# End of cross attention in a decoder: the first local row prepared in single pieces, and the last projections in the scores' PSUM

## The chip, the cores and the metric

The kernel runs on one core of one Trainium2 chip. The metric is device time in microseconds. The kernel before took a median of 3036.18 us over three runs (3035.45 to 3040.28).

## The reference, cut to what matters

Two decoder layers work on x with 8 batch rows of 512 tokens and 256 channels. The change lies between the second and the third block of the first layer:

```python
x = x + _L0_attn_ref(_layernorm(x), ...)            # self attention
x = x + _L0_xattn_ref(_layernorm(x), ctx_1024, ...) # cross attention, 16 heads of 16
x = x + _L0_ffn_ref(_layernorm(x), ...)             # local transformer: 2 x (local attention, FFN)
```

Cross attention: queries from x and keys and values from the context; a masked softmax with a factor exp(adj); an output projection; and the sum with x. The local transformer that follows takes a fresh layer norm of that sum. Each of its layers shifts half of the channels by one token and projects to q, k, v (8 heads of 64). It divides each head of q and k by its own length, turns them by rotary angles with scales, attends in windows of 128 keys, and projects back. A gated FFN follows. All arithmetic is in float32.

## The kernel before, in words

`FastDecoder` (from L1278) writes the whole program out, one stage after another, and each stage is a generator. A stage runs its first pieces while the stage ahead of it is still at work: `Ahead.step(k)` advances it by k `yield`s, until it yields `MAIN`. Then its main part begins, with PSUM pools of its own. `Background` (L3366) is a heap of small thunks with due times; `later.tick(2)` runs up to two that are due.

The program is written in this order, but a scheduler decides in which order the instructions stand on each engine. It goes by readiness and by the program's order as priority, and by when tile slots come free. `tc.issue_after(ins)` puts what a block writes behind `ins`, for the instructions of the same engine as `ins` only. `paced(thunk)` (L1707) does so with `marks[-2]`, the last multiplication on VectorE (DVE) of two steps ago. Once it is laid out, each engine works strictly in order, and so does the DMA queue of SyncE (SP). A DMA that waits holds up those behind it.

**Cross attention** (`stage_cross_attention`, L1528) runs 128 steps, 16 for each batch row: step i is four heads against 128 keys. `scores(i)` (L1724) makes four matmuls on TensorE (PE) into two tiles of two PSUM banks each (tag "sc", three such tiles). `soften(i)` takes the exponential of both tiles on ScalarE (ACT, L1735) and multiplies them by mask and adj on DVE (L1736). `weigh(i - 2)` (L1752) makes eight matmuls against the values into the bank "po". After every fourth step `po` is copied out as `x_o` (L1758, ACT). Four DMAs bring it to `x_oT` (L1766). Its sums go through DRAM to `x_sums` (L3302, L3303); `x_inv` is their reciprocal (L3306, DVE); this goes through `invs` (L3307) to `x_wide` (L1776, four DMAs). GpSimd (POOL) multiplies `x_oT` by `x_wide` (L1769). When the second group of a row is there, `project_out(b, i)` follows for four token tiles: two matmuls (L1785) into the bank "pj", an addition to x (L1790, DVE), and its statistics (L1495, L1496). After the fourth, x is written to DRAM (`away`, L1797). Newton steps for the reciprocal root (L1506 to L1508) and the normalization in place (L157) come then. The last waits for the write to `away`, since it overwrites x.

The PSUM of this stage is full: one bank "pj", one "po", six for "sc".

**Local attention's first row** is prepared during the last steps of cross attention (`prepare(0)` in `local_attention`, L1836): rotary tables, then

- `turn` (L1873): transpose x, copies on ACT into `la_hT`;
- `project(i, j)` (L1889): two matmuls for token tile i and part j (0 q, 1 k, 2 v); for q and k two reads by ACT (L1896 square, L1897 copy), for v one copy (L1894);
- `square` (L1905, DVE): sums of squares; `root` (L1913 and L1477 to L1481, DVE): 11 small instructions for two tiles;
- `rotate` (DVE): normalization (L1920), two halves with sine (L1928, L1929), cosine (L1930), sum (L1931);
- `turn_heads` (L1939, PE; L1942, ACT): transposes into `la_qkT`, in two halves of four.

All these write PSUM through `self.pj()`, which is the one bank "pj" until local attention's own pools exist. These pools lie on the same eight banks: "sum" and "po" first, then four banks of scores where the first two "sc" tiles were, then two "pj" where the third was.

The main part of local attention then begins with `scores` (L2007), whose results DVE adds a mask to (L2016), and with `prepare(1)`.

In the kernel before, the list of pieces has 18 thunks, of up to three calls each; from step 116 on, `ahead.step(3)` writes three of them per step, with no `paced` around it.

Of the kernel before, what the change touches and what calls it, by code (L numbers as in the profile page):

```python
# [27 lines left out]
F32 = mybir.dt.float32  # L28
# [6 lines left out]
ALU = mybir.AluOpType  # L35
# [4 lines left out]
P = 128  # L40
B, S, C = 8, 512, 256
# [1236 lines left out]
class FastDecoder(Decoder):  # L1278
# [249 lines left out]
    def stage_cross_attention(self, ahead):  # L1528
# [6 lines left out]
        nc, t = self.nc, self.t  # L1535
# [6 lines left out]
        first = early.enter_context(self.tc.tile_pool(reuse_waits="tile", name="xa0", bufs=2, side="right"))  # L1542
# [154 lines left out]
        with self.tc.tile_pool(reuse_waits="tile", name="xa", bufs=2) as pool, self.tc.tile_pool(  # L1697
# [9 lines left out]
            def paced(thunk):  # L1707

                with self.tc.issue_after(marks[-2]):
                    thunk()  # L1710

            def scores(n):
                b, rest = divmod(n, 16)
                G, kt = divmod(rest, 4)
                g, e = divmod(G, 2)
                d = held[b]
                d.setdefault("e", {})[rest] = pair = []
                for p in range(2):
                    pair.append(self.alloc(psum, [P, 2, 512], F32, "sc", bufs=3))

                for m in self.together(4):
                    r = (m + 2) % 4
                    rows = slice(32 * r, 32 * r + 32)
                    nc.tensor.matmul(  # L1724
                        pair[r // 2][:, r % 2, :], d["k"][rows, g, kt * P : (kt + 1) * P], d["q"][rows, e, g, :],
                        start=True, stop=True,
                    )

            def soften(n):
                b, rest = divmod(n, 16)  # L1730
                kt = rest % 4
                d = held[b]
                for p in range(2):
                    ex = self.alloc(pool, [P, 2, 512], F32, "x_e", bufs=6)
                    nc.scalar.activation(ex, d["e"][rest][p], AF.Exp)  # L1735
                    nc.vector.tensor_tensor(  # L1736
                        ex, ex, d["share"][:, kt, :].unsqueeze(1).broadcast_to([P, 2, 512]), ALU.mult
                    )
                    d["e"][rest][p] = ex
                marks.append(self.newest(mybir.EngineType.DVE))  # L1740
# [41 lines left out]
            def project_out(b, i):  # L1782
# [13 lines left out]
                if i == NST - 1:  # L1796
# [3 lines left out]
                    for k, normal in enumerate(normals):  # L1800
                        later.add(5 + k // 2, lambda normal=normal: paced(normal))

            n = 16 * B
            ready = None
            for i in range(n + 2):
                if i < n:
                    if i % 16 == 0:
                        ready = prepare(i // 16 + 1) if i // 16 + 1 < B else iter(())
                    scores(i)
                    soften(i)  # L1810
                if i >= 2:
                    weigh(i - 2)

                for thunk in next(ready, ()):
                    if len(marks) > 1:
                        paced(thunk)
                    else:
                        thunk()
                later.tick(2)
                if i == 1:  # L1820
                    ahead.step()
                if i == n - 14:
                    early.close()
                if i >= n - 12:
                    ahead.step(3)
            ahead.step(100)
            later.drain()

    def residual(self, pool, b):
        x = self.alloc(pool, [P, NST, C], F32, "lf_x")
# [3 lines left out]
    def local_attention(self, l, y, ahead):  # L1836
# [3 lines left out]
        nc, t = self.nc, self.t  # L1840
# [6 lines left out]
        first = early.enter_context(self.tc.tile_pool(reuse_waits="tile", name="la0", bufs=2, side=sides[0]))  # L1847
# [8 lines left out]
        for i in range(NST):  # L1856
            c, s = tab["cos"][:, i], tab["sin"][:, i]
# [55 lines left out]
            nc.vector.tensor_scalar(ss, ss, 1e-24, None, ALU.max)  # L1913
            self.rsqrt(first, rn, ss, "la_rt")

        def rotate(b, i):
            d = held[b]
            qk, rn = d["rows", i], d["rn"][:, i % 2, :]
            q3 = qk.rearrange("p (h d) -> p h d", d=64)
            nc.vector.tensor_tensor(  # L1920
                q3, q3, rn.unsqueeze(2).broadcast_to([P, 16, 64]), ALU.mult
            )
            q4 = qk.rearrange("p (j h d) -> p j h d", j=2, d=64)
            r = self.alloc(first, [P, 2 * S], F32, "la_r", bufs=1)
            r4 = r.rearrange("p (j h d) -> p j h d", j=2, d=64)
            cos = tab["cos"][:, i].unsqueeze(2).broadcast_to([P, 2, 8, 64])
            sin = tab["sin"][:, i].unsqueeze(2).broadcast_to([P, 2, 8, 64])
            nc.vector.tensor_tensor(r4[..., :32], q4[..., 32:], sin[..., :32], ALU.mult)  # L1928
            nc.vector.tensor_tensor(r4[..., 32:], q4[..., :32], sin[..., 32:], ALU.mult)  # L1929
            nc.vector.tensor_tensor(q4, q4, cos, ALU.mult)  # L1930
            nc.vector.tensor_tensor(qk, qk, r, ALU.add)  # L1931

        def turn_heads(b, i):
            d = held[b]
# [12 lines left out]
        def prepare(b):  # L1947

            def one(*calls):
                def thunk():  # L1950
                    for f, *args in calls:
                        f(b, *args)
                return thunk

            p, t, s, r = project, turn_heads, square, rotate
            return [
                [one((turn, 0)), one((turn, 1)), one((p, 0, 0)), one((p, 0, 1), (s, 0))],
                [one((p, 1, 0)), one((p, 1, 1), (s, 1), (root,))],
                [one((p, 2, 0), (r, 0)), one((p, 2, 1))],
                [one((p, 3, 0), (r, 1)), one((p, 3, 1))],  # L1960
                [one((p, 0, 2), (s, 2)), one((t, 0), (s, 3), (root,))],
                [one((p, 1, 2), (r, 2)), one((t, 1))],
                [one((p, 2, 2), (r, 3)), one((t, 2))],
                [one((p, 3, 2)), one((t, 3))],
            ]
# [3 lines left out]
        for thunks in prepare(0):  # L1969
            for thunk in thunks:  # L1970
                thunk()
                yield
        yield Ahead.MAIN

        with self.tc.tile_pool(
# [4 lines left out]
            one, two = [P, 512], [P, 2, 512]  # L1980
# [97 lines left out]
            n = 8 * B  # L2078
            ahead.step()
            for pair in range(0, n + 2, 2):  # L2080
                if pair < n:
                    if pair % 8 == 0:
                        ready = prepare(pair // 8 + 1) if pair // 8 + 1 < B else [()] * 8
                    scores(pair // 2)
                if pair >= 2:
                    weigh(pair // 2 - 1)
                for i in (pair, pair + 1):
                    with self.in_turn():
                        later.tick(1)
                    if i < n:  # L2090
                        for thunk in ready[i % 8]:
                            with self.in_turn():
                                thunk()
                                later.tick(1)
                    if i == n - 6:
                        early.close()
                    if i > n - 6:
                        with self.in_turn():
                            ahead.step()
# [1477 lines left out]
```

## Time and profile before

| What | Value |
|---|---|
| median of three runs | 3036.18 us |
| profiled execution, its own time | 3039.56 us |
| span of that execution | 3037.8 us |
| PE busy | 2832.6 us (93%) |
| DVE busy | 2039.3 us (67%) |
| ACT busy | 1191.5 us (39%) |
| PE busy from 600 to 700 us | 77.64 us, granted clock 0.82 |
| PE busy from 500 to 600 us | 94.48 us, granted clock 1.00 |
| PE busy from 700 to 800 us | 93.25 us, granted clock 0.97 |

In a row of the profile, a group has the engine, the line of the kernel, the operation, what is written and what is read, and the count. A bracket holds the idle time ahead of it on its engine and who ended that idle time. A granted clock of 1.00 means that TensorE had all its pulses; at 0.50 a matmul takes twice as long. In the table by stretches, the busy time of an engine can hold part of a wait, when the wait belongs to the instruction. "Row 6" and "row 7" below are the last two batch rows of cross attention; "row 0" and "row 1" are the first two of local attention.

### The profile page before, as it was taken

How to read it: one execution, taken by the hardware profiler on the slowest of the kernel's cores; microseconds unless marked ns; L12 is line 12 of the kernel's file. 1: busy time of each engine (PE TensorE's matmuls, PEld its weight loads, DVE VectorE, ACT ScalarE, POOL GpSimd, SP SyncE). 2: the span in 40 equal slices, each digit the busy share in tenths (PEclk: the TensorE clock that was granted, in tenths of full speed). 3: DMA queues.
4: the chain of work that ended last, by engine and by line, in shares of the span. 5: the costliest groups of instructions: out<-in, count | busy, mean ns of one | idle time of the engine just before them, and what ended most of it. 6: DMA issues, size and time to landing. Idle time of an engine off the chain costs nothing. (4 is left out here: it accounts for less than half of the span.)

```text
span 3037.8 us, 39774 instructions
## 1 busy us (share of the span) xinstructions
PE 2832.6 (93%) x14929; PEld 1511.4 (50%) x14944; DVE 2039.3 (67%) x4546; ACT 1191.5 (39%) x1687; POOL 388.1 (13%) x357
## 2 busy tenths in 40 slices
PE   8999999979999999999999989998796999997998
PEld 5653333225555556555555556564444344444665
DVE  7458998977776784356776788548797766664110
ACT  2237776744444431124444431113364444441111
POOL 1111111100011110000101111101211012121111
PEclk9999999988999999999999999999897999997999
DMA  7011212101000011001000011001332132313331
GB/s 246 1 35 50 72 51 62 42 18 57 15 23 23 15 32 36 0 1 37 22 22 17 21 46 63 21 7 63 106 132 91 43 105 78 112 58 97 102 140 61
DMA packets 130694, 168.71 MB, mean 56 GB/s; under 512 B 51761, under 2 KB 79666, under 8 KB 128443
## 3 DMA queue, kind: packets, MB, share of 16 engines
q1 hardware_dynamic: 126394, 154.48, 16.3%
q0 software_dynamic: 4096, 11.59, 1.0%
q8 instruction: 119, 1.95, 0.3%
q14 instruction: 85, 0.69, 0.1%
HBM read 113.12 MB, written 47.50 MB: 53 GB/s over the span
## 5 line engine op out<-in xcount | busy, mean ns | idle before, releaser
L1889 PE MATMUL pj<-w,la_hT 128*128 128x512 f32 x720 | 334.2, 605 | 5.2 <-ACT la_qkT L1942 4.5
L1736 DVE TENSOR_TENSOR x_e<-x_e,x_share 128x1024 f32<-128x1024 f32 x256 | 315.9, 1277 | 14.3 <-ACT x_e L1735 14.1
L1735 ACT ACTIVATE x_e<-sc 128x1024 f32<-128x1024 f32 x256 | 249.2, 1023 | 83.8 <-PE sc L1724 83.8
L1889 PEld LDWEIGHTS pj<-w,la_hT 128*128 128x128 f32 x720 | 132.6, 191 | 153.4 <-issue 115.6
L2016 DVE TENSOR_TENSOR la_e<-sc,la_mask 128x1024 f32<-128x1024 f32 (+1 forms) x128 | 135.3, 1084 | 103.6 <-PE sc L2007 103.6
L3320 POOL TENSOR_TENSOR la_oT<-la_o,x_wide 128x512 f32<-128x512 f32 x64 | 97.7, 1538 | 753.1 <-DMA x_wide<-invs 678.6
L2945 ACT ACTIVATE ma_e<-sc,ma_bias 128x1024 f32<-128x1024 f32 x128 | 135.6, 1110 | 145.9 <-PE sc L2939 131.4
L2233 ACT ACTIVATE lf_gate<-pj,lf_b 128x512 f32<-128x512 f32 (+1 forms) x82 | 56.3, 687 | 333.3 <-PE pj L2212 318.0
L2020 ACT ACTIVATE la_e<-la_e 128x1024 f32<-128x1024 f32 (+1 forms) x128 | 117.5, 946 | 152.6 <-DVE la_e L2016 151.6
L2212 PE MATMUL pj<-lf_hnT,w 128*128 128x512 f32 (+1 forms) x368 | 171.4, 593 | 2.0 <-DVE lf_hid L2238 2.0
L1752 PE MATMUL po<-x_e,x_v 128*32 128x512 f32 x1024 | 140.7, 622 | 33.7 <-DVE x_e L1736 29.7
L2212 PE MATMUL sc<-lf_hnT,w 128*128 128x512 f32 x336 | 157.7, 592 | 0.0
L1724 PE MATMUL sc<-x_q,x_k 32*128 32x512 f32 x1024 | 152.9, 647 | 1.7 <-DVE sa_ok L1448 1.4
L2284 PE MATMUL po<-w,lf_hid 128*128 128x256 f32 x640 | 149.0, 379 | 0.0
L2238 DVE SCALAR_TENSOR_TENSOR lf_hid<-sc,lf_b,lf_gate 128x512 f32<-128x512 f32 x70 | 52.4, 749 | 136.4 <-PE sc L2212 133.4
L2027 PE MATMUL po<-la_e,la_v 128*64 128x256 f32 (+1 forms) x1024 | 125.8, 370 | 7.0 <-ACT la_o L2044 6.3
L2007 PE MATMUL sc<-la_qkT 64*128 64x256 f32 (+1 forms) x1024 | 128.9, 375 | 1.2 <-DVE la_e L2016 0.6
L2284 PEld LDWEIGHTS po<-w,lf_hid 128*128 128x128 f32 x640 | 117.8, 190 | 21.2 <-issue 7.4
L2939 PE MATMUL sc<-ma_qT,ma_kT 64*128 64x512 f32 x512 | 127.3, 615 | 0.4 <-ACT ma_e L2945 0.4
L2962 PE MATMUL po<-ma_e,ma_v 128*64 128x512 f32 x512 | 125.7, 612 | 0.0
L2070 PE MATMUL pj<-w,la_oT 128*128 128x256 f32 x512 | 121.0, 383 | 2.0 <-DVE lf_t L1480 0.7
L1905 DVE TENSOR_REDUCE la_ss<-la_sq 128x16 f32<-128x1024 f32 x64 | 77.7, 1215 | 65.8 <-ACT la_sq L1896 65.8
(500 smaller groups left out, 5173.6 us busy)
## 6 DMA issues: line engine op xcount, KB each, us to landing
x_wide<-invs SPq DMA_DIRECT2D x184, 128.0 KB
w<-in_f_w_dram SPq DMA_DIRECT2D x16, 1024.0 KB
kv<-kv_o SPq DMA_DIRECT2D x56, 256.0 KB
slots<-x_empty SPq DMA_DIRECT2D x8, 1028.0 KB
x_mask<-in_x_maskT_dram SPq DMA_DIRECT2D x8, 1024.0 KB
ma_kT<-kv SPq DMA_DIRECT2D x8, 1024.0 KB
ma_v<-kv SPq DMA_DIRECT2D x8, 1024.0 KB
ex_rows<-slots SPq DMA_DIRECT2D x7, 1028.0 KB
```

Of the source, the lines that this page charges most:

```text
L1724: nc.tensor.matmul(pair[r // 2][:, r % 2, :], d["k"][rows, g, kt * P : (kt + 1) * P], d["q"][rows, e, g, :], start=True, stop=True,)
L1735: nc.scalar.activation(ex, d["e"][rest][p], AF.Exp)
L1736: nc.vector.tensor_tensor(ex, ex, d["share"][:, kt, :].unsqueeze(1).broadcast_to([P, 2, 512]), ALU.mult)
L1752: nc.tensor.matmul(d["po"][32 * r : 32 * r + 32, :], d["v"][:, kt, 8 * g + 2 * r + e, :], ex[r // 2][:, r % 2, :], start=(kt == 0), stop=( ...
L1889: nc.tensor.matmul(ps, d["hT"][:, k, i * P : (i + 1) * P], wqkv[:, k, j * S : (j + 1) * S], start=(k == 0), stop=(k == 1),)
L2007: nc.tensor.matmul(both[half][:, r, jj * 256 : jj * 256 + to - j * P], d["qkT"][rows, 4 + c, j * P : (j + 1) * P], d["qkT"][rows, c, j * P ...
L2016: nc.vector.tensor_tensor(ex[:, :, :n_cols], ps[:, :, :n_cols], mask[:, :n_cols].unsqueeze(1).broadcast_to([P, 2, n_cols]), ALU.add,)
L2027: nc.tensor.matmul(out[:, j * P : to], lhsT(j), ex[:, jj * 256 : jj * 256 + to - j * P], start=(j == 0), stop=(j == 3), skip_group_check=True,
L2212: nc.tensor.matmul(ps[:m, :], w1[:, k, at : at + m], held[b]["hnT"][:, k, :], start=(k == 0), stop=(k == 1))
L2284: nc.tensor.matmul(ps[:, :C], held[b]["hid"][:, f, i * P : (i + 1) * P], w2[:, f, :], start=(f == 0), stop=False,)
L2939: nc.tensor.matmul(both[m // 2][:, r, :], d["k"][rows, c, kt * P : (kt + 1) * P], d["q"][rows, c, :], start=True, stop=True,)
L2945: nc.scalar.activation(ex, ps, AF.Exp, bias=bias[:, b * NST + kt : b * NST + kt + 1], scale=0.125)
```

## The change

There are three parts, all in the last steps of cross attention.

1. `prepare(0)` of the first local attention gives 36 thunks of one call each in a new order. A rotation is cut in three calls: normalization, the two sine halves, and cosine with sum.
2. The pieces are written from step 115 on, not 116: two per step, not three. They stand inside `paced`, so that their DVE instructions stand behind the multiplication of two steps ago.
3. From step 127 on, `self.pj()` gives a slot of the tag "pj" once in four times, and a tile of the tag "sc" (its first half) the other three times.

```diff
+            turns = iter(range(10**6))
+            def at_end():
+                if next(turns) % 4 == 0:
+                    return self.alloc(psum, [P, 512], F32, "pj")
+                return self.alloc(psum, [P, 2, 512], F32, "sc", bufs=3)[:, 0, :]
...
-                if i >= n - 12:
-                    ahead.step(3)
+                if i >= n - 13:
+                    paced(lambda: ahead.step(2))
+                if i == n - 1:
+                    self.pj = at_end
...
-        def rotate(b, i):
+        def rotate(b, i, pieces=(0, 1, 2)):
...
+            if 0 in pieces:
+                nc.vector.tensor_tensor(
+                    q3, q3, rn.unsqueeze(2).broadcast_to([P, 16, 64]), ALU.mult
+                )
+            if 1 in pieces:
+                d["r"] = self.alloc(first, [P, 2 * S], F32, "la_r", bufs=1)
+                r4 = d["r"].rearrange("p (j h d) -> p j h d", j=2, d=64)
+                nc.vector.tensor_tensor(r4[..., :32], q4[..., 32:], sin[..., :32], ALU.mult)
+                nc.vector.tensor_tensor(r4[..., 32:], q4[..., :32], sin[..., 32:], ALU.mult)
+            if 2 in pieces:
+                nc.vector.tensor_tensor(q4, q4, cos, ALU.mult)
+                nc.vector.tensor_tensor(qk, qk, d["r"], ALU.add)
...
+            if b == 0 and l == 0:
+                calls = [
+                    (turn, 0), (turn, 1), (p, 0, 0), (p, 0, 1), (p, 1, 0), (s, 0), (p, 1, 1), (s, 1), (root,),
+                    (p, 2, 0), (r, 0, (0,)), (p, 2, 1), (r, 0, (1,)), (p, 3, 0), (r, 0, (2,)), (p, 3, 1),
+                    (r, 1, (0,)), (t, 0), (r, 1, (1,)), (s, 2), (p, 0, 2), (r, 1, (2,)), (s, 3), (root,),
+                    (t, 1), (r, 2, (0,)), (p, 1, 2), (r, 2, (1,)), (p, 2, 2), (r, 2, (2,)), (r, 3, (0,)),
+                    (p, 3, 2), (t, 2), (r, 3, (1,)), (r, 3, (2,)), (t, 3),
+                ]
+                return [[one(call)] for call in calls]
```

`p`, `t`, `s` and `r` are `project`, `turn_heads`, `square` and `rotate`; the first number is the token tile.

## The prediction

> **What bounds the kernel at this place.** I read the windows table first, by tens of microseconds over the hand-over from cross attention to the first local attention. Columns: stretch, length, then busy time of PE, PE weight loads, DVE, ACT, POOL, then the granted TensorE clock, DMA share and GB/s.
>
> ```profile
> 620.00:630.00 10.00, 10.00 (x57) 2.77 (x56) 9.59 (x19) 7.98 (x12) 0.00 (x0) 1.00 0.06 15
> 630.00:640.00 10.00, 6.36 (x28) 1.82 (x24) 10.00 (x11) 5.92 (x8) 0.00 (x0) 1.00 0.00 1
> 640.00:650.00 10.00, 9.32 (x40) 2.78 (x40) 9.62 (x19) 3.69 (x5) 0.00 (x0) 0.66 0.05 12
> 650.00:660.00 10.00, 3.87 (x25) 0.79 (x21) 9.97 (x9) 2.43 (x3) 1.67 (x1) 0.86 0.07 19
> ...
> 680.00:690.00 10.00, 7.90 (x17) 4.69 (x16) 4.98 (x18) 0.00 (x0) 0.76 (x4) 0.50 0.09 36
> 690.00:700.00 10.00, 8.46 (x23) 5.04 (x22) 6.39 (x27) 0.00 (x0) 0.00 (x0) 0.50 0.14 34
> ```
>
> Three regimes are visible. Up to 630 PE is full: one step of the loop (scores, one projection, weighting) every 3.98 us. From 630 to about 665 DVE is full and PE is not: DVE is the limit. From 665 to 700 neither is: that is a chain. The timeline of PE shows the second and third regime row by row (start, length, work; in brackets the idle time ahead of it and who ended it):
>
> ```profile
> 628.26 1.06 PE L1752 MATMUL po<-x_e,x_v 128*32 128x512 f32 x8
> ...
> 633.81 1.06 PE L1752 MATMUL po<-x_e,x_v 128*32 128x512 f32 x8 [1.50 <-DVE x_e L1736]
> ...
> 640.68 1.94 PE L1752 MATMUL po<-x_e,x_v 128*32 128x512 f32 x8 [2.82 <-DVE x_e L1736]
> ...
> 658.12 1.94 PE L1752 MATMUL po<-x_e,x_v 128*32 128x512 f32 x8 [6.13 <-DVE x_e L1736]
> ...
> 665.03 1.07 PE L1752 MATMUL po<-x_e,x_v 128*32 128x512 f32 x8
> ...
> 678.00 2.07 PE L1785 MATMUL pj<-w,x_oT 128*128 128x256 f32 x4 [0.68 <-ACT la_qkT L1942]
> 680.59 2.07 PE L1785 MATMUL pj<-w,x_oT 128*128 128x256 f32 x4 [0.51 <-DVE x L1790]
> ...
> 696.13 2.07 PE L1785 MATMUL pj<-w,x_oT 128*128 128x256 f32 x4 [0.52 <-DVE x L1790]
> 698.13 3.36 PE L2007 MATMUL sc<-la_qkT 64*128 64x256 f32 x16
> ```
>
> The weighting waits for the x_e multiplication, which stands on DVE behind whole rotations. After the last weighting (665.03), the eight output projections of rows 6 and 7 go one by one through the single pj bank, 2.59 us each at half clock: 8 x 2.59 = 20.1 us, from 678.00 to 698.13. And local attention starts still later, as the timeline of DVE shows:
>
> ```profile
> 706.35 1.39 DVE L157 TENSOR_SCALAR x<-x,lt_ln_mean,lt_ln_rstd 128x256 f32<-128x256 f32 x4 [4.77 <-DMA away<-x]
> 707.65 1.22 DVE L1905 TENSOR_REDUCE la_ss<-la_sq 128x16 f32<-128x1024 f32 x1
> 708.78 2.08 DVE L2016 TENSOR_TENSOR la_e<-sc,la_mask 128x1024 f32<-128x1024 f32 x2
> ```
>
> So the end of this stage is 708.78, the first mask addition L2016. It stands on DVE behind row 7's normalization, which waits for the write to `away`, issued when the last projection has been added.
>
> **The change, part by part.** I take the order in which the changed kernel's instructions stand on each engine and fill it with the durations above. The instructions are the same ones; behind the start of local attention the order is the same on all engines; on POOL it is the same throughout. So only this window counts. Start is common: DVE reaches the x_e pair at 605.92 in both, behind the rotary tables, whose wait for la_scale (2.22 us) stays, because the DMAs stand alike on SP up to there.
>
> Step lengths used, each from back-to-back starts: x_e pair 2.28 (1.14 each), square sum 1.13, root 11 x 0.225 = 2.47, rotation 1.14 + 2 x 0.60 + 2 x 1.14 = 4.6, projection of the local row 1.92, weighting or scores 1.0 to 1.07, row projection L1785 1.06 at full clock and 2.07 at half.
>
> *1. Up to 628.* The local row's first transposition moves one step earlier. It fills PE's idle 2.60 us at 601 to 604, but the weightings still run at 3.98 us a step, so 628.26 stays: worth 0. If PE were not the limit there it would be worth up to 1.9.
>
> *2. The last six weightings.* Before: 628.26 to 665.03, 36.8 us. In the new order DVE gives, from the pair at 617.5 (the reciprocal ahead waits until 615.0 for its sums, as now): pair 619.8, square 620.9, root 623.4, normalization 624.5, pair 626.8, rotation 630.3, pair 632.6, normalization and reciprocal 633.9, pair 636.2, two sines 637.4, and only then L1790 of row 6's first projection, 637.8. That last one is the new wait. Row 6's four projections now stand inside the loop, in the single pj bank, and the bank is emptied by DVE, in order. Behind it on PE stand the local projection, the next scores, and all after them: PE idles 633.7 to 637.9, 4.2 us. It comes back with the third such projection, behind a rotation, a square and a root: 650.2 to 655.1, 4.9 us. The other two wait under 1 us. At full clock the last weighting then starts at 659.1, six us earlier than now.
>
> Here the clock decides. The Trainium skill (TensorE: Matmul & The Clock Gate, Part 1: The HAM clock gate) says that one idle window of about 3.4 us puts the array at half clock, until about 3.4 us of work release it. This speaks against the change: both new gaps are longer. The trace goes further: the gap of 2.82 us already gave a weighting of 1.94 in place of 1.06, and half clock to 647; the one of 6.13 gave 5.7 us of it. So by the rows both gaps cost: local projection +1.9, scores +1.0 behind the first; projection +1.9, weighting +0.9, L1785 +1.0 behind the second. Sum +6, last weighting at about 665.5. With gaps under the rule it would be 659.1. I take 665.5 because 4.2 and 4.9 lie between two gaps that both halved it; so this part is worth 0 (6 at most, -4 if half clock lasts to the end).
>
> *3. Behind the last weighting.* Now: x_o ends 666.74; reciprocal 673.06 (it waits for DMA); POOL multiplies at 677.93, 4.87 later; then the 20.1 us. In the new order, from x_o at 666.8: row 7's four projections use separate banks, and their first halves are done ahead. On SP `away` of row 6 stands behind the first of four x_oT copies, but its addition is done (665.7), so nothing waits. The reciprocal, though, now stands on DVE behind the last two rotations without normalization, row 6's statistics and its normalization: 665.7 + 9.6 = 675.3; `away` is issued at 667.3 and lands 5.5 later (688.32 to 693.87 now), 672.8, so it is hidden, by 2.5 us; four L157 at 0.34, then the reciprocal at 676.8, 3.7 later than now. Multiplication 676.8 + 4.87 = 681.7, end 682.9. Four closing matmuls at half clock, 2.07/4 each: 685.0; last addition 686.0 (now 698.66). Row 7's DMA to `away` as now, behind w1's load, 698.72 to 706.35 = 7.6, and 0.3 to issue: 693.9. L157 1.3 and square 1.13 as now: L2016 at 696.4 against 708.78, **12.4 us less**. The square's own input, two projections of the next row, is ready 4.6 us after their start at about 688, so it is covered by 1 us.
>
> Row 6's four additions, statistics and Newton steps (about 8.5 us on DVE) move from a time when DVE had nothing to do (6.80 and 1.49 us waits) to one when it is the limit; steps 2 and 3 contain that.
>
> *4. Afterwards.* PE is 92 to 96% busy in each 100 us from 700 to 1100, in the same order; loads are issued by the work, so the shift carries on. Unknown: 2 us either way, from where a clock window falls.
>
> Sum against its own execution: 3039.56 us, span 3037.8, gives 3027.1 and 3025.4. That execution is 3.4 above the median of the three runs, 3036.18; the saving is applied to the median: 3036.18 - 12.4 = 3023.8, with half a microsecond for a clock that recovers between the gaps: **3023.3**.
>
> **The rivals.** *A, clock stays up* (0.12): the gaps come out shorter, since a DVE row may overlap more. Last weighting 659.1, x_o 660.8, last rotation 670.3, reciprocal 671.7, L2016 691.5: 17.3 us less, 3019. For it: PE is full between the gaps. Against: the two rows of 1.94.
>
> *B, half the gain* (0.17): the pj bank costs more. Each of four hand-overs that slips by one x_e pair and a root piece, about 1.5 us, takes 6 us: 3030. For it: two of four already wait over 4 us. Against: later ones have DVE work that was due anyway.
>
> *C, no change* (0.07): the end is given by something not in this count, for instance DVE catching up with row 1's rotations (DVE is full at 720 to 730), so that an early start is waited away: 3034 to 3038. Against: that work is the same and starts with the same event.
>
> *D, slower* (0.06): the same hand-over, one mechanism. From 628 on PE runs through six weightings with four projections whose bank DVE must empty. If each costs more than 3.1 us beyond the count (4 x 3.1 = 12.4), the gain is gone; at 5 us, as when each addition stands behind a full rotation or root and the array stays at half clock, it is 20 us, 3044. For it: the order does put additions behind such pieces twice. Against: the DVE work up to the last x_e multiplication is about 4 us less than now (one and a half rotations moved behind it, additions added), so PE cannot be held longer than DVE is full.
>
> **How the numbers follow.** My case has 0.58, 3018 to 3027. Three runs lie within 4.8 us, so about 0.2% (6 us) can be told from no change. Faster: 0.58 + 0.12 + nearly all of B = 0.86; same: C and the edge of B, 0.08; slower 0.06. Range 3015 to 3031: A's 3019 less 2 and a bit, B's end; C and D stay out.
>
> **What would show it.** L1785 of row 6 between the last weightings; two PE gaps of 4 to 5 us ahead of local projections, ended by DVE L1790, half clock behind both; last weighting at 665; eight serial projections gone; reciprocal of row 7 near 677, L2016 near 696. Wrong if the last weighting is past 675, or if the reciprocal waits for `away`, or if local attention's next row is not ready.

## The result and the profile after

The changed kernel takes 3024.47 us (median of 9 runs, 3020.36 to 3029.2) against 3036.18 us beside it (9 runs, 3030.28 to 3041.62): ratio 0.996, 95% interval 0.995 to 0.9971, that is 11.7 us less by the medians. Forecast were 3023.3 us: 12.4 us less by the sum, and half a microsecond more as an allowance for the clock. The profiled execution takes 3023.1 us, span 3021.3, which is 16.5 us below the profiled execution of before. So the size is right, but the profiled pair differs by 4 us more than the sum had it, and that has to be explained too.

The windows table of the changed kernel comes first (columns as in the table of before: stretch, length, busy time of PE, weight loads, DVE, ACT, POOL, granted clock, DMA share, GB/s):

```profile
630.00:640.00 10.00, 4.31 (x12) 1.33 (x12) 10.00 (x14) 0.63 (x1) 1.72 (x1) 0.67 0.06 14
640.00:650.00 10.00, 9.91 (x65) 3.61 (x64) 7.66 (x10) 8.42 (x11) 0.42 (x1) 0.98 0.07 17
650.00:660.00 10.00, 6.08 (x24) 2.16 (x24) 9.09 (x22) 0.69 (x2) 0.00 (x0) 0.83 0.07 14
660.00:670.00 10.00, 9.17 (x45) 4.88 (x38) 9.79 (x26) 4.45 (x9) 0.10 (x1) 1.00 0.20 67
670.00:680.00 10.00, 4.92 (x17) 3.50 (x15) 2.67 (x10) 1.02 (x2) 2.75 (x6) 0.72 0.08 16
680.00:690.00 10.00, 9.71 (x40) 5.32 (x39) 4.85 (x23) 3.71 (x7) 0.00 (x0) 0.94 0.78 264
690.00:700.00 10.00, 8.69 (x45) 4.63 (x44) 9.25 (x19) 7.11 (x12) 0.00 (x0) 1.00 0.00 0
```

The three regimes are there again. DVE is full to nearly full from 630 to 670, with one slack stretch (7.66 from 640). What is gone is the long time at clock 0.50: before had it from 680 to 700, and behind 660 there is now only the stretch from 670 that is low (0.72). The two low stretches ahead (0.67 and 0.83) hold the gaps of the next table. The burst of loads for the next stage (264 GB/s) stands at 680; before it came at 700.

The timeline of PE in the changed kernel (start, length, work; the bracket holds the idle time ahead and who ended it):

```profile
626.49 1.07 PE L1752 MATMUL po<-x_e,x_v 128*32 128x512 f32 x8
...
631.72 1.06 PE L1752 MATMUL po<-x_e,x_v 128*32 128x512 f32 x8 [2.03 <-DVE x_e L1736]
636.75 3.74 PE L1897 MATMUL pj<-w,la_hT 128*128 128x512 f32 x4 [3.97 <-DVE x L1790]
640.42 1.14 PE L1724 MATMUL sc<-x_q,x_k 32*128 32x512 f32 x8
...
654.07 3.61 PE L1897 MATMUL pj<-w,la_hT 128*128 128x512 f32 x4 [3.92 <-DVE x L1790]
657.62 1.06 PE L1752 MATMUL po<-x_e,x_v 128*32 128x512 f32 x8
...
659.67 1.07 PE L1752 MATMUL po<-x_e,x_v 128*32 128x512 f32 x8
...
676.86 1.22 PE L1785 MATMUL sc<-w,x_oT 128*128 128x256 f32 x2 [5.08 <-POOL x_oT L1769]
...
678.72 1.91 PE L1785 MATMUL sc<-w,x_oT 128*128 128x256 f32 x4
680.57 2.12 PE L2027 MATMUL sc<-la_qkT 64*128 64x256 f32 x16
```

The two hand-overs of the pj bank show as gaps of 3.97 and 3.92 us, both ended by the addition L1790. Half clock covers just the one projection behind each (3.74 and 3.61 in place of 1.98). The next scores (1.14) and the next weighting (1.06) are at full clock again; in the two later profiles of this kernel these rows take up to 0.23 us longer. Between the end of GpSimd's multiplication (676.80) and the first scores of local attention there are now 3.7 us of closing projections (676.86 to 680.57); eight serial projections, one every 2.59 us, stood there before. The timeline of DVE shows the chain around it:

```profile
669.28 1.38 DVE L157 TENSOR_SCALAR x<-x,lt_ln_mean,lt_ln_rstd 128x256 f32<-128x256 f32 x4
670.57 0.25 DVE L3326 RECIPROCAL x_inv<-x_sums 128x16 f32<-128x16 f32 x1
...
680.68 0.42 DVE L1790 TENSOR_TENSOR x<-x,sc 128x256 f32<-128x256 f32 x1
688.76 1.38 DVE L157 TENSOR_SCALAR x<-x,lt_ln_mean,lt_ln_rstd 128x256 f32<-128x256 f32 x4 [4.73 <-DMA away<-x]
690.05 1.21 DVE L1913 TENSOR_REDUCE la_ss<-la_sq 128x16 f32<-128x1024 f32 x1
691.18 2.08 DVE L2036 TENSOR_TENSOR la_e<-sc,la_mask 128x1024 f32<-128x1024 f32 x2
```

Row 6's normalization (669.28) has no wait in brackets: its write to `away` has landed. The reciprocal of row 7 stands right behind it. The end of the stage, the first mask addition, is at 691.18 in place of 708.78.

Whole executions start this window up to 4 us apart, so the runs below are compared from a common mark: the seventh weighting from the end (626.49 here, 628.26 in before), the last row up to which PE is full in every kernel. Times from that mark, each from the kernel's timelines, "third scores" being the third group of L2027 (L2007 in before):

| Kernel | last weighting | reciprocal of row 7 | first mask addition | third scores | whole profiled execution |
|---|---|---|---|---|---|
| before | 36.77 | 44.80 | 80.52 | 92.24 | 3039.56 |
| before, second profile | 35.69 | 43.70 | 80.99 | 92.71 | 3042.36 |
| changed | 33.18 | 44.08 | 64.69 | 76.41 | 3023.10 |
| changed, second profile | 33.84 | 44.75 | 65.28 | 76.99 | 3024.27 |
| changed, third profile | 33.52 | 44.43 | 65.20 | 76.92 | 3025.91 |
| PSUM alone | 35.48 | 43.49 | 74.88 | 86.60 | 3032.04 |
| pieces alone | 33.53 | 44.43 | 71.26 | 82.98 | 3027.04 |
| unpaced | 36.28 | 46.41 | 65.73 | 77.45 | 3028.43 |
| additions first | 34.52 | 44.75 | 63.86 | 75.57 | 3021.39 |
| `away` first | 33.61 | 44.52 | 59.65 | 75.80 | 3022.54 |
| reciprocal first | 33.65 | 41.99 | 61.77 | 73.49 | 3016.64 |
| reciprocal first, second profile | 33.88 | 42.22 | 61.63 | 73.34 | 3023.55 |
| reciprocal and `away` first | 33.60 | 41.94 | 56.82 | 72.58 | 3017.98 |
| all three | 34.45 | 43.74 | 58.20 | 73.70 | 3022.65 |

Profiles of the same kernel lie up to 1.1 us apart in the first two columns and up to 0.6 in the next two, so smaller differences between two rows say nothing.

The reciprocal of row 7 comes at the same time in before and after, for different reasons. In before, DVE stood idle until its sums had come; in the changed kernel it stands right behind other work of DVE (669.28 above). The row of before:

```profile
673.06 0.25 DVE L3306 RECIPROCAL x_inv<-x_sums 128x16 f32<-128x16 f32 x1 [7.99 <-DMA x_sums<-sums]
```

All the gain, 80.76 - 65.06 = 15.7 us on the means, comes behind this reciprocal.

### The profile page after: what moved, and what is told of

The parts are those of the page before. It is cut to its first block, busy times and chain, and to the rows that moved or that the text cites. A ratio compares the mean times of both kernels' runs of the same rounds, so it can differ in the third digit from the quotient of the medians.

```text
span 3021.3 us, 39786 instructions
## 1 busy us (share of the span) xinstructions
PE 2819.4 (93%) x14944; PEld 1507.2 (50%) x14944; DVE 2034.0 (67%) x4546; ACT 1192.4 (39%) x1687; POOL 386.9 (13%) x357
## 5 line engine op out<-in xcount | busy, mean ns | idle before, releaser
L2027 PE MATMUL sc<-la_qkT 64*128 64x256 f32 (+1 forms) x1024 | 128.0, 373 | 2.5 <-DVE la_e L2036 1.9
```

The lines of the kernel that those rows point to most:

```text
L2027: nc.tensor.matmul(both[half][:, r, jj * 256 : jj * 256 + to - j * P], d["qkT"][rows, 4 + c, j * P : (j + 1) * P], d["qkT"][rows, c, j * P ...
```

## The experiments

My theory: PSUM banks for row 7 and pieces behind the multiplications each carry part of the gain. The rivals: one of the two parts does all, the clock decides, or DVE's work alone sets the end whatever the order.

### The PSUM part alone

The kernel before with only the third part of the change:

```diff
+            turns = iter(range(10**7))
+            def at_end():
+                if next(turns) % 4 == 0:
+                    return self.alloc(psum, [P, 512], F32, "pj")
+                return self.alloc(psum, [P, 2, 512], F32, "sc", bufs=3)[:, 0, :]
...
                 if i >= n - 12:
                     ahead.step(3)
+                if i == n - 1:
+                    self.pj = at_end
```

> The kernel before, and only the last part of the change: from step 127 on, pieces that ask for a bank get the scores' PSUM three times in four. Theory (the gain comes from taking the eight output projections out of one bank behind the last weighting): row 6 still goes one by one through pj, 4 x 2.59 us, row 7 no longer: the first local scores start near 690.5 in place of 698.1, the time is 7 to 8 us under the kernel before. Rival (the gain comes from the single pieces, which free DVE for the x_e multiplications): the last weighting stays at 665 and the time stays within 2 us of the kernel before.

Measured: 3032.54 us, ratio 0.9986 (0.9976 to 0.9995); first mask addition 5.9 us earlier than the mean of before's two profiles. The medians differ by 3.7 us, where the theory had 7 to 8: the first local scores are at 693.74, not near 690.5. From its timeline of PE:

```profile
662.95 1.03 PE L1785 MATMUL sc<-w,x_oT 128*128 128x256 f32 x4
...
681.87 2.08 PE L1785 MATMUL pj<-w,x_oT 128*128 128x256 f32 x4 [0.58 <-DVE x L1790]
...
689.63 2.07 PE L1785 MATMUL pj<-w,x_oT 128*128 128x256 f32 x4 [0.51 <-DVE x L1790]
691.50 2.31 PE L1785 MATMUL sc<-w,x_oT 128*128 128x256 f32 x6
```

Three first halves of row 7 are done early, in the scores' PSUM (the first two at 662.95). But row 6's four projections still go one by one through pj, up to 689, and so does row 7's first, which needs pj too (689.63). Row 7's other three closing halves stand behind it in order (691.50). So row 7 takes 4.1 us behind row 6, where the theory left about 2, and banks alone give about a third of the gain.

### The pieces alone

The changed kernel without the third part (`self.pj = at_end` taken out).

> The changed kernel without its last part: single pieces, two per step and paced, but all in the one bank pj to the end. Theory: the last weighting as in the changed kernel (start near 660), row 6's projections inside the loop, but row 7's four one by one behind the POOL multiplication, 4 x 2.59 = 10.4 us in place of about 4: 6 us slower than the changed kernel, 6 to 9 us faster than the kernel before. Rival (single pieces make the whole gain): as fast as the changed kernel.

Measured: 3028.92 us, ratio 0.9973 (0.9965 to 0.9981); first mask addition 9.5 us earlier than before. The two gaps are those of the changed kernel (3.97 and 3.92), the last weighting and the reciprocal too. The difference is behind the multiplication, where row 7's four go through the one bank:

```profile
678.07 2.05 PE L1785 MATMUL pj<-w,x_oT 128*128 128x256 f32 x4 [0.72 <-POOL x_oT L1769]
680.63 2.07 PE L1785 MATMUL pj<-w,x_oT 128*128 128x256 f32 x4 [0.51 <-DVE x L1790]
...
685.81 2.07 PE L1785 MATMUL pj<-w,x_oT 128*128 128x256 f32 x4 [0.51 <-DVE x L1790]
```

Four times 2.59 are 10.4 us, against 4.3 in the changed kernel (676.80, the end of the multiplication, to 681.10, the end of the last addition), so 6.1; the first mask addition is 71.26 - 65.06 = 6.2 later than there. With the two parts measured apart, 5.9 and 9.5 us, the sum is 15.4 of the 15.7 that both give together. By the medians the two are worth 3.7 and 7.3 us, together 11.0, beside the 11.7 of the result. Neither does it all, and the two simply add. The rival of the clock is not apart from this. The eight projections of before took 2.07 us each where the same work takes 1.06 at full clock, so some 8 of their 20 us are half clock (an estimate from these rows). They went with the chain that held them; no run here tells the two apart.

### Without the pacing

```diff
-                    paced(lambda: ahead.step(2))
+                    ahead.step(2)
```

> The changed kernel without paced around the two pieces of each step; nothing is left out. Theory (cutting the pieces small and giving them in the new order is what brings the x_e multiplications earlier; the pacing adds nothing to an order that goes by readiness): last weighting within 1 us of 659.7, two gaps of about 4 us behind the output projections again, time within 0.1% of the changed kernel. Rival (the pacing is what keeps the pieces behind the multiplications): rotations stand ahead of x_e multiplications as before, last weighting near 665, time near 3029.

Measured: 3024.37 us, ratio 0.9957 (0.9947 to 0.9968); the changed kernel beside it 3024.27, ratio 0.9958 (0.9944 to 0.9971). So the time is the theory's, but the rows are not what it said:

```profile
642.88 3.78 PE L1897 MATMUL pj<-w,la_hT 128*128 128x512 f32 x4 [7.49 <-DVE x L1790]
646.59 2.09 PE L1724 MATMUL sc<-x_q,x_k 32*128 32x512 f32 x8
...
659.92 1.93 PE L1752 MATMUL po<-x_e,x_v 128*32 128x512 f32 x8 [2.96 <-DVE x_e L1736]
```

In place of two gaps of 4 us there is one of 7.49 and one of 2.96, and the last weighting is 2.8 us later than the mean of the changed kernel (36.28 against 33.51; at 665.50, where the rival had it). Yet the first mask addition is only 0.7 later (65.73 against 65.06). From the last weighting to the reciprocal it is 10.1 us in place of 10.9, since fewer rotations are left there (the reciprocal waits 0.22 us for its sums, not for DVE); and from the reciprocal to the mask addition 19.3 in place of 20.6, since the first closing projections run at full clock (0.70 where they took 1.22). Pacing moves the waits about, and the end stays where it was.

### What follows row 6's additions stands behind them

The two gaps wait for an addition that stands on DVE behind other work. Here the exponentials' multiplications and the pieces of the next step are put behind the newest of row 6's additions:

```diff
+            def after_add():
+                return self.tc.issue_after(behind[0]) if behind else nullcontext()
...
                 nc.vector.tensor_tensor(x, x, ps[:, :C], ALU.add)
+                if b == B - 2:
+                    behind[:] = [self.newest(mybir.EngineType.DVE)]
...
-                    soften(i)
+                    with after_add():
+                        soften(i)
...
-                    paced(lambda: ahead.step(2))
+                    with after_add():
+                        paced(lambda: ahead.step(2))
```

> The changed kernel, with what follows a row-6 addition on DVE (the next x_e pair, the next pieces) put behind that addition, so that the pj bank is emptied sooner. Theory (the two PE gaps of 3.9 us and the half clock behind them are partly on the path, DVE is the limit else): gaps under 2 us, no half clock behind them, last weighting 2 to 3 us earlier, reciprocal of row 7 near 668 in place of 670.6; 2 to 4 us faster than the changed kernel. Rival 1 (DVE alone is the limit, gaps are covered): the same within 1 us. Rival 2 (clock is all of it): 5 us or more faster.

Measured: 3021.97 us, ratio 0.9953 (0.9937 to 0.9969), not told apart from the changed kernel's 0.996. The gaps are nearly gone. The first projection is at half clock all the same; so was the weighting ahead of it (632.02, 1.93 us), which follows a gap of 2.52 us:

```profile
634.72 3.78 PE L1905 MATMUL pj<-w,la_hT 128*128 128x512 f32 x4 [0.77 <-DVE x L1794]
...
648.79 1.98 PE L1905 MATMUL pj<-w,la_hT 128*128 128x512 f32 x4 [0.62 <-DVE x L1794]
```

The last weighting comes no earlier for it, but 1 us later than in the changed kernel (34.52 against 33.51), and the reciprocal stands at 44.75 against 44.42. So closing PE's gaps did not bring the reciprocal forward. That speaks for the rival in which DVE's work is the limit here: between the mark and the reciprocal, DVE of the changed kernel idles only 2 to 3 of 44 us. But the two hand-overs are not shown to be free, since this order brought DVE a wait of its own, in which it idles for a reciprocal's sums:

```profile
648.21 0.25 DVE L3334 RECIPROCAL x_inv<-x_sums 128x16 f32<-128x16 f32 x1 [3.08 <-DMA x_sums<-sums]
```

The first mask addition is 1.2 us earlier (63.86 against 65.06), because the first closing projections run at full clock (0.70 where they took 1.22).

### The write to `away` ahead of the next stage's loads

```diff
                     nc.sync.dma_start(self.away[b], self.x[:, b * NST : (b + 1) * NST, :])
+                    self.away_last = self.newest(mybir.EngineType.SP)
...
             n = 8 * B
-            ahead.step()
+            with self.tc.issue_after(self.away_last) if l == 0 else nullcontext():
+                ahead.step()
```

> The changed kernel, with the load of the next weights (w1, 1.4 MB) put behind row 7's write to away on SP's queue instead of ahead of it. Theory (that write takes 7.6 us because the load stands ahead of it): it lands about 2 us sooner, row 7's normalization starts at 686.5 in place of 688.8, then the square is late (its input is there at 688.4): first mask addition 1.5 us earlier, 1.5 us faster than the changed kernel. Rival (the write takes as long on its own): the same within 0.5 us in the trace.

Measured: 3023.52 us, ratio 0.9965 (0.9951 to 0.9979): not told apart from the changed kernel. The timeline of SP's queue (SPq) and then that of DVE in this kernel:

```profile
682.87 0.34 SPq L1797 DMA_DIRECT2D away<-x  x1
683.25 0.43 SPq L113 DMA_DIRECT2D w<-in_c_w_dram  x1
...
686.14 1.38 DVE L157 TENSOR_SCALAR x<-x,lt_ln_mean,lt_ln_rstd 128x256 f32<-128x256 f32 x4 [0.38 <-DMA away<-x]
687.44 2.08 DVE L2037 TENSOR_TENSOR la_e<-sc,la_mask 128x1024 f32<-128x1024 f32 x2
691.18 1.22 DVE L1914 TENSOR_REDUCE la_ss<-la_sq 128x16 f32<-128x1024 f32 x1 [1.66 <-ACT la_sq L1905]
```

From the issue to the normalization it is 3.3 us (682.87 to 686.14) where it was 7.6 behind the load of w1: 4.3 us, twice what the theory had. The first mask addition moves by even more (59.65 against 65.06), since the square sum, 1.1 us, now stands behind it and no longer ahead. But that sum is then not ready, and DVE waits 1.66 us for it. PE is filled with the next row's projections: from the first scores to the third it idles 0.29 us in this kernel, and only 1.31 us more in the changed one. So the third scores come 1.0 us earlier (75.80 against a mean of 76.77), and that is what counts. The first mask addition, the end mark of my prediction, is a good mark only as long as the work behind it moves along.

### The reciprocal ahead of row 6's normalization

Row 6's Newton steps and normalization are put behind row 7's reciprocal:

```diff
+                    self.late = roots + normals if b == B - 2 else []
+                    if self.late:
+                        return
                     for k, root in enumerate(roots):
...
             nc.vector.reciprocal(inv, small)
             nc.sync.dma_start(self.invs[at].rearrange("r (a c) -> (r a) c", c=16), inv)
+            if at == 31:
+                last = self.newest(mybir.EngineType.DVE)
...
+                for piece in self.late:
+                    with self.tc.issue_after(last):
+                        piece()
```

> The changed kernel, with row 6's Newton steps and normalization standing on DVE behind the reciprocal of row 7's sums; nothing is left out. Theory (row 6's small instructions hold up the chain to row 7's last projections by 2.4 us, and what comes after follows): reciprocal near 668.2 in place of 670.6, multiplication on GpSimd near 673.2, first mask addition 2.4 us earlier than in the changed kernel (near 688.8), time near 3022. Rival (the write to away, the next row's projections or another chain sets what follows): the reciprocal comes earlier, the third scores of local attention does not, and the time stays at 3024.

Measured: 3017.64 us (6 runs), ratio 0.9946 (0.9925 to 0.9967), with the changed kernel at 3024.27 beside it. From its timelines of DVE, POOL and PE:

```profile
667.96 0.24 DVE L3329 RECIPROCAL x_inv<-x_sums 128x16 f32<-128x16 f32 x1
668.12 0.10 DVE L1499 COPY lt_ln_mean<-lt_ln_mv 128x4 f32<-128x4 f32 x1
...
672.91 1.26 POOL L1769 TENSOR_TENSOR x_oT<-x_oT,x_wide 128x512 f32<-128x512 f32 x1 [5.62 <-DMA x_wide<-invs]
...
674.23 0.70 PE L1785 MATMUL sc<-w,x_oT 128*128 128x256 f32 x2 [2.52 <-POOL x_oT L1769]
```

The reciprocal stands 2.3 us earlier (42.1 against 44.4 from the mark), the third scores 3.4 (73.4 against 76.8). The theory's 2.4 are confirmed as the wait; the last 1 us comes from shorter closing projections, 0.70 where they were 1.22 at the lower clock. The 6.6 us between the two medians are more than the window shows, so this was measured again:

> The kernel that puts row 6's Newton steps behind row 7's reciprocal, unchanged, once more, to see whether the 6.6 us below the changed kernel stand. Theory (the window gains what its rows show, some 3 us, and the rest was scatter): first mask addition near 688, time 3019 to 3022. Rival (the whole 6 us repeat, so something behind the window gains too): time 3016 to 3018.5.

Measured: 3022.31 us, ratio 0.9948 (0.9936 to 0.9961), beside it the changed kernel at 3026.45, so 4.1 less; here the six runs of the one (up to 3023.7) and the six of the other (from 3024.9) do not overlap. The first mask addition is at 690.32, not near 688, as this execution was 2.7 us later at the mark than the first; from the mark it repeats to 0.2. Over both, 12 runs have a median of 3021.4 against 3025.1 of the changed kernel's 26: 3.7, which fits the 3.4 of the window. The rest of the first 6.6 was scatter. This version is ahead of both kernels, of the changed one by about 0.1%; its intervals against before overlap those of the changed kernel.

### Combinations

The reciprocal first, and `away` first:

> The same kernel with the write to away on SP ahead of the next stage's first load; nothing is left out. Theory (the 4 us of that wait are off the path, since the next row's projections and squares set the pace behind the first scores): third scores of local attention within 1.5 us of 699.5, time within 2 us of the kernel without it. Rival (with row 7's projections done earlier, the wait is on the path): third scores near 696, time 3 to 4 us below it.

Measured: 3021.57 us, ratio 0.9948 (0.9936 to 0.9961), as without it. Third scores 72.6 against 73.4, at 700.43 within the theory's 1.5 us of 699.5: what the wait for `away` costs here is under 1 us.

All three orders together:

> The changed kernel with three orders at once: what follows row 6's additions on DVE stands behind them, the write to away stands on SP ahead of the next stage's first load, and row 6's Newton steps stand behind row 7's reciprocal; nothing is left out. Theory A (each of them is on the path): first mask addition near 684, third scores of local attention near 698 in place of 702.9, time near 3018. Theory B (behind the first scores of local attention the pace is PE's own, with the next row's projections, so the sum of them is worth no more than the earlier end of the output projections): first mask addition near 685, third scores near 700 to 701, time 3021 to 3023.

Measured: 3021.99 us, ratio 0.995 (0.9932 to 0.9969). Theory B: first mask addition at 58.20, third scores at 73.70, no better than the reciprocal alone. Making the additions first delays the last weighting (34.45) and with it the reciprocal (43.74).

### The two kernels again

Both unchanged, to see what repeats.

> The changed kernel, unchanged, once more. Theory (the window's order and waits are fixed, and the profiled pair's 16.5 us against the medians' 11.7 is the scatter of whole executions): first mask addition within 1.5 us of 691.2, time within 2 us of 3024.5. Rival (the window itself differs from execution to execution, by where the half clock falls): last weighting or first mask addition 3 us or more off.

> The changed kernel, unchanged, beside the other two on the same chip: 3022 to 3026; first mask addition within 1 us of 691.2.

> The kernel before, unchanged, profiled once more, for the length of its window from the first weighting that the change touches (628.26 in its profile) to the first mask addition (708.78), 80.5 us; the changed kernel shows 64.7, 65.3 and 65.2 us in three profiled executions. Theory (the window's length is fixed by the order, and the medians' smaller difference is the scatter of what lies around it): 80 to 81 us again. Rival (the first profile of before was a long one, by a half clock that does not fall so each time): 77 to 78 us, which is what the medians' 12 us would make.

Measured: the changed kernel 3024.27 us, ratio 0.9958 (0.9944 to 0.9971), and 3026.45, ratio 0.9963 (0.9951 to 0.9976). From the mark to the first mask addition it took 65.28 and 65.20 us after 64.69. Counted from the start of the program, the third profile had that addition at 694.09, 2.9 from the 691.2 expected, because its whole execution was 2.4 us late at the mark. Before's window took 80.99 after 80.52. So the order fixes the window to within 0.6 us, and its difference is 15.7 us, while the medians of the three measurements differ by 11.7, 15.0 and 12.5.

The rest of the difference isn't in the rows outside the window: those take 2957.3 and 2959.6 us in before (span less window), and 2956.6, 2957.1 and 2958.9 in the changed kernel. What the runs do show is that before's executions scatter with the clock. Over 75 of them, those with a mean granted clock of 0.972 average 3042.1 us (8 runs) and those with 0.977 average 3033.7 (15 runs). Both profiled executions of before had 0.972, those of the changed kernel 0.977. Over all measurements, the median of 84 runs of before is 3037.2 and that of 26 of the changed kernel 3025.1, 12.1 less. That a typical execution of before has a shorter window than these two was not seen, and stays open; in the kernel with PSUM alone, whose first steps are before's, the same row had another clock than in these two (below).

## Why the prediction was right, step by step

**Step 1, up to 628: worth 0.** Right. Seventh weightings stand at 628.26 and 629.67 in before, and at 626.49, 626.26 and 628.89 after; PE is full ahead of them in both. Counted from a weighting ahead of all that is moved (592.75 in before, 591.48 in the changed kernel), this row comes after 35.5 and 35.3 us in before and after 35.0, 35.3 and 34.7 in the changed kernel, so at most 0.4 on the means.

**Step 2, the last six weightings: worth 0.** The mechanism was right, the size was not. Forecast gaps of 4.2 and 4.9 us, measured 3.97 and 3.92, both ended by L1790 as said. The mis-sized term is the half clock behind them: charged +6 over five groups (the five add up to 6.7, and 665.5 is 6.4 behind 659.1), measured +1.8 and +1.6 over two, so 3.4. The last weighting is at 33.5 from the mark, 2.7 us earlier than before (36.2), not 0.4 later. "D, slower" and "B, half the gain" rested on a dearer hand-over and fell with it. The experiment with the additions first adds that closing the gaps does not bring the reciprocal forward; what a hand-over costs by itself was not measured.

The Trainium skill (TensorE: Matmul & The Clock Gate, Part 1: The HAM clock gate) gives the release as about 3.4 us of work, and that agrees within some tenths with the 3.74 and 3.61 us of half-clock projection here. It does not hold everywhere: in the unpaced kernel the projection and the scores behind the gap of 7.49 us are both slow, 5.9 us in all (3.78 and 2.09). The prediction took the longest half-clock stretches of before. Rival A, with the clock up throughout, had the last weighting at 30.8 (659.1 less 628.26); the measured 33.5 lies between it and my 37.2.

**Step 3, behind the last weighting: 12.4 less.** The path was right, and its parts nearly so. Reciprocal 11.3 us behind the last weighting, measured 10.9; to the multiplication 4.87, measured 4.97; last addition 20.5 behind the last weighting, measured 21.0; `away` to the normalization 7.6, measured 7.64 (681.12 to 688.76); the write of row 6 hidden, the next row's square covered. The closing projections were mis-sized: 2.1 us summed, 3.7 measured, because a closing half is two matmuls in the rows (x2), eight for four tiles, not four. It was offset: the last addition starts 0.1 us behind the last of them, where 1.0 had been summed. (The 20.1 us of before, written as 8 x 2.59, which is 20.7, are the measured time from 678.00 to 698.13.) Together from the last weighting to the first mask addition 30.9 forecast, 31.5 measured, where it had been 43.75 (44.5 on the mean of two profiles). The named marks, reciprocal near 677 and first mask addition near 696, came at 670.57 and 691.18; 1.8 us of that is the earlier mark of this execution, most of the rest the over-charged clock of step 2.

**Step 4, the shift carries on.** Right within what can be seen: the rows outside the window take the same time, within the 2.3 us by which two executions of one kernel differ. But that the forecast comes so close to the median is in part luck. The window saved 15.7 where the sum said 12.4, and the medians 11.7 to 15.0. Two errors of about 3 us, an over-charged clock and profiled executions of before that lie above their median (3039.56 and 3042.36 against 3037.2), point opposite ways.

**C, no change** fell with all measurements.

## What to carry to other kernels

A chain is shortened where it is serial: the whole gain lay behind the reciprocal, whose own time did not move, since the earlier multiplications were used up by work that took their place in front of it. Where one engine was full, closing the gaps of another, or reordering who waits, did not bring the end of its work forward here; what did was to take work out of the full engine's queue ahead of the one instruction that a long chain hangs on (here 2.3 us of small steps ahead of a reciprocal, 3.4 us gained in the window). And check an end mark by one further behind: the first mask addition moved by 5 us in a run in which the third scores moved by 1.

## What was unexpected of the hardware

The same gap of PE does not give the same clock. Behind an idle time of 2.82 us at the same place of the program, the weighting was at half clock in both profiles of before (1.94), and at full clock in the kernel with PSUM alone, where half clock came over 1 us later, on the two rows behind. From the timeline of PE in before, and then in the kernel with PSUM alone:

```profile
640.68 1.94 PE L1752 MATMUL po<-x_e,x_v 128*32 128x512 f32 x8 [2.82 <-DVE x_e L1736]
642.54 2.09 PE L1724 MATMUL sc<-x_q,x_k 32*128 32x512 f32 x8
```

```profile
640.53 1.06 PE L1752 MATMUL po<-x_e,x_v 128*32 128x512 f32 x8 [2.82 <-DVE x_e L1736]
641.52 1.67 PE L1724 MATMUL sc<-x_q,x_k 32*128 32x512 f32 x8
643.12 3.11 PE L1899 MATMUL pj<-w,la_hT 128*128 128x512 f32 x4
```

In the second profile of the reciprocal-first kernel a gap of 2.19 us was enough (weighting 1.94), while at the same step gaps of 2.03, 2.59 and 2.31 us left it at 1.06 in the three profiles of the changed kernel. The same section of the skill says that the activity window runs freely, so that the same kernel can meet it at different phases; that would fit, but its idle window of about 3.4 us does not, since 2.19 and 2.82 us gave half clock. The length of one idle time does not tell the clock behind it, nor when half clock begins. That the phase of such a window is the cause is argued from the page, not shown. A rival for the first pair is not excluded: in both profiles of before, PE had idled 1.50 and 1.69 us one step earlier, with PSUM alone only 0.28. For a forecast, charging every row behind a gap, as I did, is the upper end of the price and not its middle.
